# Second graph's features in place of zero products, weight combinations on GpSimd, and a third visit in two parts

## The chip, the cores and the metric

The kernel runs on one core of a Trainium2 chip. Its engines run beside each other and wait for one another by semaphores: TensorE (PE, with its weight loads PEld) multiplies matrices into PSUM, VectorE (DVE) and ScalarE (ACT) work on PSUM and SBUF, GpSimd (POOL) works on SBUF, SyncE (SP) issues DMAs. The metric is the time on the device in microseconds (us). Three runs of the kernel before gave a median of 2787.26 us (2787.23 to 2788.1).

## The reference

Two layers over 64 graphs of 256 nodes with 512 features, all in float32. Layer 0 is a graph attention with 8 heads of 64 units, layer 1 a dot-product attention to which the adjacency is added. Both add their input and end in a layer normalization. The mask is all ones, and `adjacency_mat` and `distance_mat` of layer 1 are both `adj`.

```python
# layer 0
feats = einsum('bnf,hfu->bhnu', x, W)
e_self, e_neigh = einsum('bhnu,hu->bhn', feats, a_self), einsum('bhnu,hu->bhn', feats, a_neigh)
dense = leaky_relu(e_self[..., :, None] + e_neigh[..., None, :], 0.2) - 1e10 * (1 - adj)
x = layernorm(x + relu(einsum('bhij,bhju->bhiu', softmax(dense), feats) + b))
# layer 1
q, k, v = split(x @ W_qkv)
attn = softmax(q @ k.T / 8, masked) * 0.33 + 0.33 * adj + 0.33 * exp(-adj)
x = layernorm(x + (attn @ v) @ W_out + b_out)
```

## The kernel before

**Tiling.** A graph's 256 nodes are T = 2 tiles of 128 rows. The 512 features are C = 4 tiles. Heads come in two groups of HG = 4. Every matmul is issued as two halves of 64 columns (`halved`, L82 to 87), so most PE rows of the profile carry L87 whatever they belong to.

**Seven products.** From graph 2 on, and for q, k, v and the output projection of every graph, a product of 2 x 2 blocks is done with seven block products in place of eight (`seven`, `seven_rows`). They are called p1 to p7. Each needs a sum of blocks of its left side (`left_factors`, the tiles xC, hC, oC, on DVE) and a combination of blocks of the weights. The seven results lie in three PSUM banks: "alone" (p2), "pair" (p5, then p3) and "chain" (p1, p6, p7, p4 one on top of the other). ACT copies the chain bank out after each of its four products, and the next one of the chain waits for that copy. `add` (`qk_add`, `v_add`) adds another bank on DVE.

**Weight combinations.** They are made once, in the start: `combine` (L286 to 299) for q and k, four instructions of 128x1024; `right_factors` (L235 to 247) for v (`wv_sb`, through `CW[0](3)`), for layer 0 (`wf_sb`) and for the output projection (`wo_sb`), four instructions each of 128x512 or 128x528. All sixteen are on DVE.

**Layer 0 of a graph** (`proj0`, `attend0`). For graphs 0 and 1 `features(t, g)` makes the features of a tile and a group of heads directly; `logits` and `copied` take them out of PSUM on DVE; `maxima`, `clamped`, `columns` and `factors` make the exponentials of the logits, one part as a column per head (`CCOL`), one spread over all partitions by matmuls with a selector (`GB`). `aT` transposes the adjacency block by block on DVE, and `far` makes from it two exponentials on ACT. `weights(h)` is one DVE instruction per tile (L767) that makes the unnormalized attention of head h, `scaled(h)` scales the features on ACT (L725), `product(g, t)` multiplies both on PE (L790), `rec0` and `norm0` divide, `end`, `squares` and `norm` are residual and layer normalization, with small steps on POOL (L385 to 406). `shared` makes for layer 1 the part of the attention that comes from the adjacency, on DVE. From graph 2 on the spread exponentials go through DRAM: `rows`, `shift` and `broadcast` write a row tensor gs and read it back on all partitions as gb.

**Zero products.** `keep_busy(dst, n)` (L453 to 456) issues n matmuls of zeros whose result nobody reads. The start has four places: eight in `attention_vectors`, eight and two in `maxima` for graph 0, and six in `busy` for graph 1.

**Order.** The order of the work on each engine is written out by hand: `do(stage, b, step)` runs a step, and `in_order()` chains every instruction to the one before it on its engine. Each engine works its instructions in that order, and so does SP with the DMAs. `start` does all of graph 0's layer 0 and half of graph 1's; `second_beside_first` runs graph 1 beside layer 1 of graph 0; then come, for b = 2 to 62, `attention0_beside_projections1(b)` and `attention1_beside_projections0(b)`, and `end`. The third visit of the change is the first of these two for b = 2.

**Buffers.** Tiles of one tag share as many buffers as `bufs` says. A tile's first writer waits until the last reader of the tile that it replaces is done. Single buffers that matter here: `xb` (an x in blocks, `load`), `adj` (an adjacency in blocks, `load_adj`), `adjT`, `v0` (the features of a graph), `gb`. PSUM has four slots of tag `mm` and two larger ones of tag `sc`.

**Loads.** x and adj are loaded by four DMAs each (`load_blocks`, L119 to 124) on SP, with 128-byte pieces.

Of the kernel before, what the change touches and what calls it, by code (L numbers as in the profile page):

```python
# [17 lines left out]
def kernel(  # L18
# [163 lines left out]
    load_wf(nc.sync, 1)  # L182

    sel = work.tile([P, H + 1, P], FT, tag="rb", name="sel", bufs=1)
    nc.vector.memset(sel[:, H, :], 1.0)
    load_adj(0)
# [48 lines left out]
    def right_factors(w, w12, steps=range(4)):  # L235

        w11, w21, w22, m1, m2, m3, m4 = w
        for i in steps:
            if i == 0:
                nc.vector.tensor_add(m3, w22, w12)  # L240
            elif i == 1:
                nc.vector.tensor_sub(m2, m3, w11)
            elif i == 2:
                nc.vector.tensor_sub(m1, w11, w12)
            else:
                nc.vector.tensor_sub(m4, w21, m2)
        in_order()
# [17 lines left out]
    def load_weights1():  # L265
# [20 lines left out]
        def combine(part):  # L286
            q1, q2, s1, s2, s3, s4, k2 = wqk_sb
            if part == 0:
                nc.vector.tensor_add(s1, wk1, k2)
            elif part == 4:  # L290
                nc.vector.tensor_sub(s2, s1, q1)
            elif part == 1:
                nc.vector.tensor_sub(s3, q1, wk1)
            elif part == 2:
                nc.vector.tensor_sub(s4, q2, s2)
            else:
                right_factors(wv_sb, wv12)
                return
            in_order()
# [196 lines left out]
    def proj0(b):  # L496
# [4 lines left out]
        V0[b] = work.tile([P, T, H, UX], FT, tag="v0", name=f"v0_{b}", bufs=1)  # L501
# [120 lines left out]
        def maxima(part=None):  # L622

            if part == 1:
                matmul(ROW["max"], sel[:H, H, :], ROW["diag"], start=True, stop=True)
                if b == 0:
                    keep_busy(WA[1][:, 0, :2], 2)
# [6 lines left out]
            if b == 0:  # L634
                keep_busy(WA[1][:, 0, :2], 8)
# [654 lines left out]
    def start():  # L1290
# [32 lines left out]
        for t in range(T):  # L1323
            do("proj0", 0, "features", t, 1, 3)
        do("proj0", 0, "aT")
        do("proj0", 0, "far", 0)
        CW[0] = load_weights1()
        load_adj(1)
        do("proj0", 0, "logits", 1)
        do("proj0", 0, "cleared")  # L1330
        do("proj0", 0, "maxima")
        do("proj0", 0, "copied", 0, 0)
        do("proj0", 0, "copied", 1, 0)
        do("proj0", 0, "maxima", 1)
        do("proj0", 0, "clamped")
        do("proj0", 0, "columns")
        for h in range(HG):
# [4 lines left out]
        do("proj0", 0, "factors", HG, HG)  # L1342
        for t in range(T):
            do("attend0", 0, "product", 0, t)
        do("turned", 1, "xT")
        do("proj0", 0, "copied", 0, 1)
        do("proj0", 0, "copied", 1, 1)
        load(2)
        do("attend0", 0, "rec0", 0)
        for h in range(HG, H):  # L1350
            do("proj0", 0, "scaled", h)
        masks(1)
        masks(2)
        do("attend0", 0, "norm0", 0, 0)
        do("attend0", 0, "norm0", 0, 1)
        do("proj0", 0, "far", 1)
        for t in range(T):
            do("proj0", 1, "features", t, 0)
        for h in range(HG, H):
            do("attend0", 0, "weights", h)  # L1360
        for t in range(T):
            do("attend0", 0, "product", 1, t)
        do("proj0", 1, "cleared")
        do("proj0", 1, "logits", 0)
        CW[0](0)
        do("attend0", 0, "rec0", 1)
        CW[0](4)
        for t in range(T):
            do("attend0", 0, "norm0", 1, t)
            do("proj0", 1, "features", t, 1)  # L1370
# [4 lines left out]
        do("proj0", 1, "copied", 0, 0)  # L1375
        do("proj0", 1, "copied", 1, 0)
# [12 lines left out]
        do("proj0", 0, "shared", 0)  # L1389
        do("proj0", 1, "aT")  # L1390
        CW[0](1)
        CW[0](2)
        right_factors(wf_sb, wf12, (0,))
        do("proj1", 0, "qk", "p1")
        do("proj1", 0, "from_rows", 1)
        do("proj1", 0, "blocks")
        load_rows(1)
        do("proj0", 1, "far", 0)
        do("proj1", 0, "qk", "p2")
        do("proj1", 0, "hC")  # L1400
        do("proj1", 0, "qk_add", 11)
        do("proj1", 0, "qk", "p6")
        for h in range(HG):
            do("proj0", 1, "scaled", h)
            do("attend0", 1, "weights", h)
        do("proj0", 0, "shared", 1)
# [3 lines left out]
        do("proj0", 1, "factors", HG, HG)  # L1410
        do("proj1", 0, "qk_add", 22)
        for h in range(HG, H):
            do("proj0", 1, "scaled", h)
        for h in range(HG, H):
            do("attend0", 1, "weights", h)
        do("proj0", 1, "far", 1)
        load_adj(2)
        do("proj1", 0, "qk", "p4")

    def second_beside_first():  # L1420
# [3 lines left out]
        for g in range(2):  # L1424
            for t in range(T):
                do("attend0", b, "product", g, t)
        CW[0](3)
# [18 lines left out]
        right_factors(wf_sb, wf12, (1, 2))  # L1446
# [3 lines left out]
        right_factors(wf_sb, wf12, (3,))  # L1450
# [49 lines left out]
    def attention0_beside_projections1(b):  # L1500
# [17 lines left out]
        for h in range(HG, H):  # L1518
            do("proj0", b, "scaled", h)
        do("proj1", b - 1, "qk", "p5")  # L1520
        for h in range(HG, H):
            do("attend0", b, "weights", h)
        do("proj1", b - 1, "qk", "p7")
        if 2 < b < NB - 1:
            do("turned", b + 1, "xC")
        do("proj1", b - 1, "qk_add", 22)
        for g in range(2):
            for t in range(T):
                do("attend0", b, "product", g, t)
        do("attend0", b, "rec0", 0)  # L1530
# [3 lines left out]
        if b == 2:  # L1534
            do("turned", 3, "xT")
# [3 lines left out]
        do("attend1", b - 2, "weights", 0, 1)  # L1539
        for t in range(T):  # L1540
            do("attend0", b, "norm0", 0, t)
        do("proj1", b - 1, "qk", "p4")
        for t in range(T):
            do("attend0", b, "norm0", 1, t)
        do("proj1", b - 1, "qk", "p3")
        do("attend1", b - 2, "weights", 1, 1)
        do("proj1", b - 1, "qk_add", 12)
        do("attend0", b, "end")
        do("proj1", b - 1, "values", "p1")
        do("proj1", b - 1, "values", "p2")  # L1550
        do("proj1", b - 1, "v_add", 11)
        do("attend1", b - 3, "residual")
# [3 lines left out]
        do("proj1", b - 1, "v_add", 22)  # L1556
        for t in range(T):
# [238 lines left out]
    load(1)  # L1796
# [55 lines left out]
```

## Time and profile before

| | |
|---|---|
| median of three runs | 2787.26 us |
| profiled execution | 2787.98 us |
| its span, first to last instruction | 2786.2 us |
| PE busy | 2773.7 us, 100% |
| DVE busy | 2567.0 us, 92% |
| ACT busy | 1798.0 us, 65% |
| POOL busy | 416.7 us, 15% |
| mean granted clock of TensorE | 0.999 |

A row of the timeline reads: start in us from the span's start, length in us, engine, line of the kernel, operation, output<-input by the program's names, shapes, and xN for N instructions merged into the row. In square brackets stands the idle time of the engine just before, and what ended it. Rows of groups give, after the bar, busy us and the mean ns of one instruction, then the idle time ahead of them. Rows of windows give, after the window and its length, the busy us of PE, PEld, DVE, ACT and POOL, the granted clock, the busy share of the DMA engines and GB/s. Matmuls are pipelined, so the rows of two neighbours can overlap by some 0.1 us.

### The profile page before, as it was taken

What the parts mean: (1) busy time and instruction counts of PE and PEld (TensorE: products, weight loads), DVE (VectorE), ACT (ScalarE), POOL (GpSimd) and SP (SyncE); (2) the same over time, 40 slices, a digit from 0 to 9 for tenths busy, and PEclk for the clock granted to TensorE, in tenths of its full rate; (3) what the DMA queues carried; (4) which work ended last, traced back from release to release, by engine and by line L of the source; (5) the groups of instructions that cost most, each with busy time, mean ns of one, the idle gap of its engine ahead of it and who ended that gap; (6) DMA issues with size and microseconds to landing.
All of it is one profiled execution on the core that took longest, in us unless ns stands there. A gap on an engine that the chain in (4) does not pass through costs nothing.

```text
span 2786.2 us, 93446 instructions
## 1 busy us (share of the span) xinstructions
PE 2773.7 (100%) x38576; PEld 2197.5 (79%) x38576; DVE 2567.0 (92%) x5281; ACT 1798.0 (65%) x5057; POOL 416.7 (15%) x1027
## 2 busy tenths in 40 slices
PE   9999999999999999999999999999999999999998
PEld 7778778788787887887877877878788878788786
DVE  7999999999999999999999999999999999999996
ACT  4566666666666666666666666666666666666664
POOL 1111111111111111111111111111111111111110
PEclk9999999999999999999999999999999999999999
DMA  6444545445445444454454454544544545545432
GB/s 143 124 106 138 134 128 144 124 129 142 120 136 140 124 140 124 135 146 118 133 141 120 139 131 130 145 124 128 145 116 138 138 126 142 124 132 146 116 119 80
DMA packets 778389, 362.57 MB, mean 130 GB/s; under 512 B 694767, under 2 KB 696303, under 8 KB 761966
## 3 DMA queue, kind: packets, MB, share of 16 engines
q1 hardware_dynamic: 775854, 356.07, 47.8%
q8 instruction: 306, 5.01, 0.7%
q14 instruction: 117, 0.96, 0.1%
q10 hardware_dynamic: 2112, 0.52, 0.1%
HBM read 288.11 MB, written 68.13 MB: 128 GB/s over the span
## 4 chain that ended last, share of the span: by engine, by line
PE 98%; DVE 1%; ACT 0%; DMA 0%; issue 0%; POOL 0%; SPq 0%; POOLq 0%; DVEq 0%; ACTq 0%
PE pq_p L87 28%; PE po_p L87 14%; PE pf_p L87 14%; PE pv_p L87 14%; PE av L790 9%; PE pz L951 8%; PE av L1078 8%; PE pd L988 2%; PE pf L87 0%; PE po L87 0%; DMA gb<-gs 0%; PE pg L663 0%; ACT x L811 0%; PE common L1157 0%; PE raw L1142 0%
## 5 line engine op out<-in xcount | busy, mean ns | idle before, releaser
L87 PE MATMUL pq_p<-hC,wqk_sb 128*64 128x128 f32 x8192 | 470.0, 273 | 0.5 <-ACT qk L348 0.5
L87 PEld LDWEIGHTS pq_p<-hC,wqk_sb 128*64 128x64 f32 x8192 | 448.7, 137 | 2.0 <-ACT qk L348 1.0
L767 DVE SCALAR_TENSOR_TENSOR pT<-gb,ccol,at 128x256 f32<-128x256 f32 x992 | 403.1, 478 | 17.3 <-ACT ccol L677 17.3
L87 PE MATMUL pq_p<-hT,wqk_sb 128*64 128x128 f32 x6144 | 358.2, 273 | 0.8 <-DVE hT L130 0.8
L972 ACT ACTIVATE p<-pz,hide 128x512 f32<-128x512 f32 (+1 forms) x640 | 339.3, 623 | 29.3 <-PE pz L951 29.3
L87 PEld LDWEIGHTS pq_p<-hT,wqk_sb 128*64 128x64 f32 x6144 | 342.1, 137 | 11.1 <-PE po_p L87 1.2
L1059 DVE TENSOR_TENSOR p<-p,rb 128x1024 f32<-128x1024 f32 x252 | 299.1, 1207 | 2.4 <-DMA rb<-rs 2.4
L1068 DVE TENSOR_TENSOR p<-p,ct 128x1024 f32<-128x1024 f32 x252 | 299.4, 1208 | 0.1
L811 ACT ACTIVATE x<-av,rec 128x64 f32<-128x64 f32 x1024 | 224.7, 335 | 62.2 <-DVE rec L803 62.2
L790 PE MATMUL av<-v,pT 128*64 128x65 f32 x8192 | 253.4, 222 | 1.6 <-issue 0.9
L725 ACT ACTIVATE v<-v 128x64 f32<-128x64 f32 x1024 | 251.2, 336 | 3.8 <-DVE v L716 3.7
L87 PE MATMUL pf_p<-wf_sb,xC 128*64 128x264 f32 x1984 | 253.6, 386 | 0.0
L790 PEld LDWEIGHTS av<-v,pT 128*64 128x64 f32 x8192 | 249.5, 138 | 3.9 <-issue 2.7
L402 POOL TENSOR_SCALAR rstd_l<-rstd_l 128x2 f32<-128x2 f32 (+1 forms) x128 | 93.9, 734 | 1048.8 <-ACT junk L391 1048.8
L348 ACT COPY qk<-pq_p 128x512 f32<-128x512 f32 x256 | 149.1, 582 | 153.9 <-PE pq_p L87 150.8
L87 PE MATMUL pv_p<-wv_sb,hC 128*64 128x256 f32 x2048 | 243.7, 379 | 0.0
L348 ACT COPY v<-pv_p 128x256 f32<-128x256 f32 x256 | 95.5, 373 | 223.8 <-PE pv_p L87 223.5
L951 PE MATMUL pz<-qk 64*128 64x256 f32 x2048 | 239.4, 383 | 0.0
L87 PE MATMUL po_p<-wo_sb,oC 128*64 128x256 f32 x2016 | 239.2, 379 | 0.0
L1078 PE MATMUL av<-p,v 128*64 128x256 f32 x2016 | 229.1, 379 | 0.0
L951 PEld LDWEIGHTS pz<-qk 64*128 64x128 f32 x2048 | 192.2, 186 | 45.9 <-issue 25.6
L980 DVE SCALAR_TENSOR_TENSOR both<-p 128x512 f32<-128x512 f32 x256 | 173.1, 677 | 41.4 <-ACT p L972 41.4
(181 smaller groups left out, 4549.2 us busy)
## 6 DMA issues: line engine op xcount, KB each, us to landing
rb<-rs SPq DMA_DIRECT2D x63, 1024.0 KB
gb<-gs SPq DMA_DIRECT2D x62, 1028.0 KB
hs<-x SPq DMA_DIRECT2D x64, 512.0 KB
xb<-in_x_dram SPq DMA_DIRECT2D x252, 128.0 KB
x<-in_x_dram SPq DMA_DIRECT2D x63, 512.0 KB
y<-hs SPq DMA_DIRECT2D x63, 512.0 KB
out_dram<-y SPq DMA_DIRECT2D x63, 512.0 KB
hb<-hs SPq DMA_DIRECT2D x248, 128.0 KB
```

Source lines behind the costliest of these rows:

```text
L87: matmul(dst[cols], lhsT[:, cols], rhs, **flags)
L348: nc.scalar.copy(out[COPIES[p]], dst)
L725: nc.scalar.activation(v[:, :U], v[:, :U], AF.Copy, scale=v[:, U : U + 1])
L767: nc.vector.scalar_tensor_tensor(pT[h][:, j, :], GB[b][h], CCOL[b][:, j, h : h + 1], AT[b][:, j, :], op0=ALU.max, op1=ALU.mult,)
L790: matmul(av[r * half : (r + 1) * half, k, :], pT[h][:, j, i : i + half], V0[b][:, j, h, :UA], start=(j == 0), stop=(j == T - 1),)
L811: nc.scalar.activation(X1[b][:, t, h * U : (h + 1) * U], av[:, k, :U], AF.Copy, scale=REC0[g][:, t, k : k + 1],)
L951: matmul(pz[r][:, j, :], QK[b][rows, g, 1, j * P : (j + 1) * P], QK[b][rows, g, 0, :], start=True, stop=True,)
L972: nc.scalar.activation(to, of, AF.Exp, bias=hide[:, j, b : b + 1], scale=U**-0.5)
L980: nc.vector.scalar_tensor_tensor(both[g], p[:, :, 0, :], TINY, p[:, :, 1, :], op0=ALU.add, op1=ALU.add)
L1059: nc.vector.tensor_mul(p, p, REC[b][:, k : k + 2, g // 2, :] .unsqueeze(2) .to_broadcast([P, 2, T, N]),)
L1068: nc.vector.tensor_add(p, p, CT[b].unsqueeze(1).to_broadcast([P, 2, T, N]))
L1078: matmul(av[0][r * U : (r + 1) * U, g % 2, :], V1[b][:, j, 2 * g + r, :], PROBS[b][g][:, r, j, :], start=(j == 0), stop=(j == T - 1),)
```

## The change

Five things are changed; everything from b = 3 on is as it was.

1. Graph 1's x is loaded ahead of adjacency 0 on SP (before: after it, just before `start`), and transposed (`turned`) before graph 0's maxima.
2. The eight and two zero products of `maxima` for graph 0 go. Graph 1's `features` of group 0 are issued at two places in graph 0's layer 0: tile 0 behind the maxima, tile 1 behind the factors. Graph 1's features lie in the buffer of `gb`.
3. All sixteen weight combinations are issued on POOL, those of q, k, v and layer 0 in `start`, those of the output projection where they were.
4. Steps are moved in `start`: `aT` of graph 0 behind the maxima, `aT` of graph 1 ahead of its second logits, `shared` of graph 0 into graph 0's layer 0, all eight `scaled` of graph 1 in one run.
5. For b = 2, p4 and p3 of the q/k product stand between the two groups of `product`, and the later weights, scalings and additions are ordered for that.

```diff
     load_wf(nc.sync, 1)
+    load(1)
+    load_adj(0)
...
-    load_adj(0)
...
             if i == 0:
-                nc.vector.tensor_add(m3, w22, w12)
+                nc.gpsimd.tensor_add(m3, w22, w12)
...
             if part == 0:
-                nc.vector.tensor_add(s1, wk1, k2)
+                nc.gpsimd.tensor_add(s1, wk1, k2)
...
-        V0[b] = work.tile([P, T, H, UX], FT, tag="v0", name=f"v0_{b}", bufs=1)
+        tag = "gb" if b == 1 else "v0"
+        V0[b] = work.tile([P, T, H, UX], FT, tag=tag, name=f"v0_{b}", bufs=1)
...
-                if b == 0:
-                    keep_busy(WA[1][:, 0, :2], 2)
...
-            if b == 0:
-                keep_busy(WA[1][:, 0, :2], 8)
...
             do("proj0", 0, "features", t, 1, 3)
+        do("turned", 1, "xT")
+        do("proj0", 0, "copied", 0, 0)
+        do("proj0", 0, "copied", 1, 0)
+        CW[0] = load_weights1()
+        load_adj(1)
+        do("proj0", 0, "cleared")
+        masks(1)
+        do("proj0", 0, "logits", 1)
+        do("proj0", 0, "maxima")
+        masks(2)
+        do("proj0", 1, "features", 0, 0)
         do("proj0", 0, "aT")
         do("proj0", 0, "far", 0)
...
         do("proj0", 0, "factors", HG, HG)
+        do("proj0", 1, "features", 1, 0)
         for t in range(T):
             do("attend0", 0, "product", 0, t)
...
+            do("proj0", 1, "features", t, 1)
         do("proj0", 1, "cleared")
-        do("proj0", 1, "logits", 0)
         CW[0](0)
+        CW[0](4)
         do("attend0", 0, "rec0", 1)
-        CW[0](4)
+        do("proj0", 0, "shared", 1)
...
-        do("proj0", 1, "copied", 0, 0)
-        do("proj0", 1, "copied", 1, 0)
+        do("proj0", 1, "aT")
         do("proj0", 1, "logits", 1)
...
-        right_factors(wf_sb, wf12, (0,))
+        right_factors(wf_sb, wf12)
+        CW[0](3)
+        do("proj0", 1, "far", 0)
+        do("proj0", 1, "factors", HG, HG)
+        for h in range(H):
+            do("proj0", 1, "scaled", h)
         do("proj1", 0, "qk", "p1")
         do("proj1", 0, "from_rows", 1)
         do("proj1", 0, "blocks")
+        for h in range(6):
+            do("attend0", 1, "weights", h)
...
+        for t in range(T):
+            do("attend0", b, "product", 0, t)
         do("proj1", 0, "qk", "p4")
...
         do("proj1", b - 1, "qk", "p7")
+        if b == 2:
+            do("attend0", b, "weights", HG)
+            do("proj1", b - 1, "qk_add", 22)
+            for h in range(HG + 1, H):
+                do("attend0", b, "weights", h)
+            for h in range(HG, H):
+                do("proj0", b, "scaled", h)
...
         for g in range(2):
             for t in range(T):
                 do("attend0", b, "product", g, t)
+            if b == 2 and g == 0:
+                do("proj1", 1, "qk", "p4")
+                do("proj1", 1, "qk", "p3")
+                do("proj1", 1, "qk_add", 12)
```

## The prediction

> **What bounds the kernel now.** First the page's busy table and chain, to see which engine sets the end.
>
> ```profile
> PE 2773.7 (100%) x38576; PEld 2197.5 (79%) x38576; DVE 2567.0 (92%) x5281; ACT 1798.0 (65%) x5057; POOL 416.7 (15%) x1027
> PE 98%; DVE 1%; ACT 0%; DMA 0%; issue 0%; POOL 0%; SPq 0%; POOLq 0%; DVEq 0%; ACTq 0%
> ```
>
> TensorE is idle for 12.5 us of 2786.2, 7 of them in the last 46. From graph 3's visit on the code is unchanged and PE is full. So the change can gain only what it removes of PE work and of PE stalls in the first 125 us. Next, PE in order of time at the start.
>
> ```profile
> 18.44 1.95 PE L456 MATMUL pa_bc<-rowmask 128*128 128x128 f32 x16
> ...
> 20.64 0.71 PE L456 MATMUL pa_bc<-rowmask 128*128 128x128 f32 x4
> ...
> 36.83 0.75 PE L90 MATMUL pr<-ident,lg 128*8 128x128 f32 x4
> 37.42 1.50 PE L456 MATMUL pg<-rowmask 128*128 128x128 f32 x12
> 39.06 0.66 PE L90 MATMUL ph<-ident,x 128*128 128x128 f32 x4
> ```
>
> The first two L456 rows are the zero products that go. From start to start of their followers they hold PE for 20.32-18.44 = 1.88 and 21.19-20.64 = 0.55: 2.43 us. The row at 36.83 is where the second graph's maxima begin. Last, graph 2 (the third visit), in DVE and PE order of time.
>
> ```profile
> 87.67 0.19 DVE L670 TENSOR_TENSOR nd<-v,gb 128x16 f32<-128x16 f32 x1 [1.81 <-DMA gb<-gs]
> ...
> 88.40 3.21 DVE L767 SCALAR_TENSOR_TENSOR pT<-gb,ccol,at 128x256 f32<-128x256 f32 x8
> ...
> 88.73 1.97 PE L87 MATMUL pq_p<-hC,wqk_sb 128*64 128x128 f32 x32 [0.51 <-ACT qk L348]
> ...
> 90.53 6.26 PE L790 MATMUL av<-v,pT 128*64 128x65 f32 x128
> ...
> 92.13 3.25 DVE L767 SCALAR_TENSOR_TENSOR pT<-gb,ccol,at 128x256 f32<-128x256 f32 x8
> ```
>
> The 128 products take 6.26 us; the same ones for graph 1, and in every later visit, take 3.90. PE follows DVE's weights head by head and loses 2.36 us.
>
> **The start, step by step.** Graph 1's features for group 0 (two blocks of 16 matmuls, 1.95 us each) move ahead of graph 0's maxima and of product 0; PE work is otherwise kept. They need graph 1's transposed x. Its four loads move ahead of adj 0's on SP: from the issue at 11.41-14.78 to 8.00-11.4. Counting bytes in one-microsecond windows in order of issue, all that is ahead of x 1 (1.89 MB) is through at 13.0 and x 1 (0.52 MB more) at 16.7, 1.9 us after its last issue. So x 1 lands near 13.4, and DVE, free at 15.16, transposes it (1.24) by 16.4; the two copies (0.73), the mask transpose (0.38) and the logits come before PE ends the features at 17.85. No wait. adj 0 lands near 16.3; its transpose is now wanted at 19.5: hidden, with 3 us to spare. The PSUM slots for the mask and the new features come free by those copies. The mask's two transposes (0.33) only move. Graph 1's features buffer takes the space of gb, which nothing writes before 81.87: no cost.
>
> PE would thus be 2.43 us early at 36.83, at 34.4. But DVE's transpose of adj 1, at 41.08 before, now stands ahead of logits 1 and maxima 1, and its load keeps its place on SP:
>
> ```profile
> 30.71 2.67 SPq L123 DMA_DIRECT2D adj<-in_adj_dram  x4
> ```
>
> SP is in one stream of issues from 4.6 us to 38, so nothing brings this forward: it ends at 33.38. Landing: bytes counted give 34.3, plus 1.9 us gives 35.3; I take 35.1. Then transpose (0.7) and first logits (0.2): PE starts the maxima at 36.05, not 34.4. A **new stall of 1.6 us** takes the place of two thirds of the gain; 0.78 stays, and 0.23 more since the normalized tile (L90 ph, which waited for ACT) is now early. Queued behind the waiting transpose on DVE are the logits, the maximum and the copies; PE and ACT wait for those. The parts of shared that come earlier on DVE (0.68, 0.29, 0.87 from 29.6) lie where it waits for product 1 or ACT's norm0: nothing. Start: **0.9 to 1.0 gained**; ends 0.3 (landing 35.7) and 2.4 (no wait).
>
> From there to 60 us PE order changes but not its sum. The tightest place is p6, which needs hC: ACT now does all 16 scalings (two rows of 2.02) ahead of the copies of p1 and hT. Counted from factors at 39.96 in old time: ACT is free at 45.6 (0.7 and 4.0 after its column step at 40.9), PE ends p1 at 45.7; copies 1.2 us, three sums on DVE 1.1: p6 at 48.1, where PE gets to at 48.2 (two factor blocks 3.8, p1 1.9, ph 0.6, p2 1.97). Cost 0, up to 0.5. The six weights ahead of hC (4.8 us from 41.6) end at 46.4, before hT is there.
>
> **Weights by GpSimd.** Sixteen DVE instructions go to POOL. The row for POOL is this one:
>
> ```profile
> L467 POOL TENSOR_TENSOR prod<-wf_sb,a_bc 128x512 f32<-128x512 f32 x3 | 3.5, 1192 | 5.4 <-ACT a_bc L441 5.4
> ```
>
> 1.19 us per 128x512 against DVE's 0.68. So 4 x 2.4 + 4 x 1.23 + 8 x 1.19 = 24 us on an engine that is 15% busy; DVE gets 4 x 1.2 + 4 x 0.7 + 8 x 0.68 = 13 back. The first two (s1, s2) run from 27, when their loads are down, to 31.8, and the LayerNorm step behind them on POOL is wanted at 33.1: hidden. s3, s4, wf and wv follow that step, from 36.9 to 51.4: s3 is ready at 39.3 and wanted by p7 near 49, wv at 62.66, wf at 67: hidden. The two of wo stand ahead of POOL's clearing of grow_sb, at 71.28 before and wanted by DVE at 74.0: POOL is free at 71.35, 2.38 + 0.21 gives 73.94. Just hidden; any slowing goes straight into the gb chain.
>
> Rule against this: the Trainium skill, "GPSIMD Engine Reference", Key points, says GpSimd shares its SBUF interfaces with VectorE and contends with DVE instructions that have two SBUF inputs. The row doesn't test that: beside it DVE ran L467 (one input in PSUM) and reductions, at their usual 0.68. By the row the cost is 0. By the rule the hC sums (0.42 each, both inputs in SBUF) may double, +1.1 at p6, and wo may be late by as much. I take the row and keep +2.2 for the range.
>
> **The third visit.** Weights 0 to 3 end at 91.61 in old time. Product group 0 then has a quarter of its first tile and the second left (1.2 us): 92.8. p4 and p3 (1.75 each) cover DVE's weights 4 to 7, which end at 96.0 behind both additions: PE at 96.3; group 1 (1.9) ends at 98.2, against 100.29. Gain 2.1. Off that: norm0 on ACT now falls beside the copies of the values, and p7 of these waits 0.2; and at the row sums of graph 1's softmax (124.72) PE meets DVE, which is ahead by two wo additions (1.2) and its own waits (0.5), 0.3 less than PE. **1.5 gained**; ends 0 (DVE doesn't keep up) and 2.1. The wait of 0.51 and that for gb stay: they hang on gb's DMA, which starts from PE's last product of graph 2 and moves with it.
>
> **Sum.** 0.9 + 1.5 = 2.4 us. The profiled execution took 2787.98 with a span of 2786.2 (1.8 around it): 2783.8 and 2785.6 after. Its time is 0.7 above the median shown, 2787.26, so the median would be **2784.9**.
>
> **The clock.** The stall on adj 1 stands where zero products used to keep PE going. The end of the trace shows what idleness does (windows of one microsecond; PE, PEld, DVE, ACT, POOL, clock, DMA):
>
> ```profile
> 2779.00:2780.00 1.00, 0.23 (x4) 0.00 (x0) 0.65 (x4) 0.51 (x2) 0.00 (x0) 1.00 0.00 0
> 2781.00:2782.00 1.00, 0.00 (x0) 0.00 (x0) 0.18 (x1) 0.19 (x1) 0.70 (x2) 0.78 1.03 387
> 2782.00:2783.00 1.00, 0.00 (x0) 0.00 (x0) 0.17 (x1) 0.32 (x1) 0.00 (x0) 0.50 0.08 29
> ```
>
> PE stops at 2779.23 and the clock halves near 2781.56, 2.3 us later. The skill ("TensorE: Matmul & The Clock Gate", Part 1) puts the drop at one idle window of some 3.4 us. By the page, 1.6 us of stall costs nothing; by the row, 2.3 us can be enough. The price is seen at the start, where eight zero products take 3.78 us (from 1.04) instead of 1.95, with full rate from about 6.2: some 4 us at half rate, +2. I take 0, since 1.6 is under both.
>
> **Rivals.**
> 1. No stall: adj 1 lands by 34.3, or DVE comes to it later. Start 2.4, total 3.9: 2783.4. For it: the byte count. Against it: SP's last issue at 33.38. Chance 0.15.
> 2. Slower: GpSimd's additions run beside DVE at 2.4 us per 128x512 instead of 1.19. s1 and s2 then end at 36.6, the LayerNorm of graph 0 is 3.5 late and PE waits 1.7 at ph; wo ends 2.3 late and gb with it; hC 1.1. -2.4 + 1.7 + 2.3 + 1.1 = +2.7: 2790. It turns the sign from about 1.9 us each. For it: the rule; against it: the row. Chance 0.15, with a part beyond +5.6 where more is late than I see.
> 3. The clock drops at the stall: +2 to +3 on the likeliest: 2787.4, no change. Chance 0.1.
> 4. The third visit gives nothing, DVE being the bound from gb's landing to 124 us: only the start's 0.9: 2786.4. For it: DVE's 100% in 100-110. Chance 0.15.
>
> The likeliest has 0.45, its own range 2784.0 to 2786.2. A measurement of this kernel tells about 0.2%, 5.6 us, from no change. More than that faster would need all of 2.43, 2.36 and 1.5 of other stalls: 0.03. Slower than that: half of rival 2: 0.08. Range: 2782.7 takes in rival 1; 2788.8 takes in 3, 4 and the milder part of 2.
>
> **What would show it.** The features of graph 1 at about 18.8 where L456 stood; DVE idle before L130 adjT<-adj near 34, released by DMA, and PE idle 1.6 us before pr; POOL rows of 1.19 and 2.4; av for graph 2 in two runs of about 2 to 2.3 us with pq_p between, values p1 near 97.3. Wrong if x 1 lands after 15.7, if the POOL rows are much longer, or if the clock column falls below 1.00 near 36 us.

## The result and the profile after

The changed kernel takes 2794.84 us (median of 14 runs, 2792.58 to 2797.59) against 2788.07 for the kernel before (14 runs, 2787.22 to 2790.88): a ratio of 1.0025, 95% interval 1.0017 to 1.0032. It is slower by 6.8 us, where the prediction said 2784.9 with a range up to 2788.8. The profiled execution has a span of 2793.0 us against 2786.2, also 6.8 more. First the busy table and the chain of the changed kernel:

```profile
PE 2771.4 (99%) x38556; PEld 2199.2 (79%) x38556; DVE 2564.5 (92%) x5265; ACT 1796.0 (64%) x5057; POOL 442.3 (16%) x1043
PE 97%; DVE 1%; POOL 0%; DMA 0%; ACT 0%; issue 0%; SPq 0%; POOLq 0%; DVEq 0%; ACTq 0%
```

PE is busy for 2.3 us less and still ends 6.8 us later: it is now idle for 21.6 us of its span instead of 12.5. Where that idle time is shows in PE's order of time (start, length, what; in brackets the idle time before and what ended it):

```profile
18.17 2.00 PE L87 MATMUL pf<-wf_sb,xT 128*64 128x264 f32 x16
...
32.73 1.09 PE L87 MATMUL pf<-wf_sb,xT 128*64 128x264 f32 x8
36.83 0.60 PE L90 MATMUL pr<-ident,lg 128*8 128x128 f32 x4 [3.02 <-DVE lg L615]
...
41.32 5.38 PE L661 MATMUL pg<-grow_sb,sel 128*128 128x256 f32 x16 [1.79 <-DVE nd L668]
...
53.21 5.46 PE L87 MATMUL pq_p<-hC,wqk_sb 128*64 128x128 f32 x96 [2.14 <-DVE hC L315]
...
100.96 1.74 PE L788 MATMUL av<-v,pT 128*64 128x65 f32 x53
103.39 0.51 PE L788 MATMUL av<-v,pT 128*64 128x65 f32 x10 [0.69 <-issue]
...
117.22 1.11 PE L87 MATMUL pf_p<-wf_sb,xC 128*64 128x264 f32 x8 [1.60 <-DVE v L352]
```

The features stand where the zero products stood, and PE is through with graph 1's features at 33.8. Then come three stalls that the kernel before did not have at these places, 3.02, 1.79 and 2.14 us, all released by DVE, and at 41.32 sixteen factor products that take 5.38 us instead of two blocks of 1.99. Why DVE is late shows in DVE's rows of the changed kernel beside POOL's:

```profile
28.86 2.15 DVE L529 TENSOR_TENSOR ct<-adjT,far 128x512 f32<-128x512 f32 x1
31.12 2.25 DVE L531 TENSOR_SCALAR even<-mf 128x256 f32<-128x256 f32 x1
...
38.85 2.32 DVE L644 TENSOR_SCALAR grow_sb<-grow_sb 8x256 f32<-8x256 f32 x1
...
50.17 1.49 DVE L317 TENSOR_TENSOR hC<-hT 128x256 f32<-128x256 f32 x1
51.59 1.48 DVE L315 TENSOR_TENSOR hC<-hT,hC 128x256 f32<-128x256 f32 x1
```

```profile
28.10 2.37 POOL L290 TENSOR_TENSOR wqk_sb<-wk,wqk_sb 128x1024 f32<-128x1024 f32 x1 [3.54 <-DMA wv_sb<-in_L_gnn_W_qkv_dram]
30.55 2.69 POOL L292 TENSOR_TENSOR wqk_sb<-wqk_sb,wqk_sb 128x1024 f32<-128x1024 f32 x1
...
38.68 2.35 POOL L294 TENSOR_TENSOR wqk_sb<-wqk_sb,wk 128x1024 f32<-128x1024 f32 x1
...
49.95 1.43 POOL L243 TENSOR_TENSOR wv_sb<-wv_sb,wv_sb 128x512 f32<-128x512 f32 x1
51.35 1.44 POOL L245 TENSOR_TENSOR wv_sb<-wv_sb,wv 128x512 f32<-128x512 f32 x1
```

The same four in the kernel before:

```profile
39.40 0.28 DVE L646 TENSOR_SCALAR grow_sb<-grow_sb 8x256 f32<-8x256 f32 x1 [0.30 <-ACT grow_sb L640]
...
40.16 0.68 DVE L527 TENSOR_TENSOR ct<-adjT,far 128x512 f32<-128x512 f32 x1
40.87 0.29 DVE L529 TENSOR_SCALAR even<-mf 128x256 f32<-128x256 f32 x1
...
45.77 0.42 DVE L314 TENSOR_TENSOR hC<-hT,hC 128x256 f32<-128x256 f32 x1
```

Add start and length in the changed kernel: POOL's 30.55 row ends at 33.24 and DVE's 31.12 row (`even`) at 33.37; POOL's 38.68 row ends at 41.03 and DVE's 38.85 row (the clamp, 8 rows by 256 elements) at 41.17. The clamp goes from 0.28 to 2.32, `even` from 0.29 to 2.25, `ct` from 0.68 to 2.15, the hC sums from 0.42 to 1.5. The POOL rows beside them last 2.4 to 2.7 and 1.4 us. So certain DVE instructions wait for the end of GpSimd's instruction, whatever their own size.

### The profile page after: what moved, and what is told of

Its sections match the earlier page's. It is cut to its first block, busy times and chain, and to the rows that moved or that the text cites. A ratio compares the mean times of both kernels' runs of the same rounds, so it can differ in the third digit from the quotient of the medians.

```text
span 2793.0 us, 93415 instructions
## 1 busy us (share of the span) xinstructions
PE 2771.4 (99%) x38556; PEld 2199.2 (79%) x38556; DVE 2564.5 (92%) x5265; ACT 1796.0 (64%) x5057; POOL 442.3 (16%) x1043
## 4 chain that ended last, share of the span: by engine, by line
PE 97%; DVE 1%; POOL 0%; DMA 0%; ACT 0%; issue 0%; SPq 0%; POOLq 0%; DVEq 0%; ACTq 0%
PE pq_p L87 28%; PE po_p L87 14%; PE pv_p L87 14%; PE pf_p L87 14%; PE av L788 8%; PE pz L949 8%; PE av L1076 8%; PE pd L986 2%; DVE pT L765 0%; PE pf L87 0%; PE po L87 0%; PE pg L661 0%; DMA gb<-gs 0%; PE common L1155 0%; PE raw L1140 0%
```

## The experiments

Four theories were at stake. **The lock**: while GpSimd works on SBUF, a DVE instruction of a certain kind stands still until GpSimd's ends, and this is the loss. **Bandwidth**: the two engines share one, so each slows the other in proportion. **The order**: the moved steps (adj 1's transpose ahead of logits 1, weights ahead of hC) are the loss. **The clock**: its fall to half rate behind the new stalls is the loss. Letters in the expectations are those that each expectation defines.

Runs that were made together share their runs of the kernel before. All times in us.

| run | median | before's, made together | ratio, 95% |
|---|---|---|---|
| dve_back | 2791.44 | 2789.32 | 1.0007 [0.9999, 1.0016] |
| pool_only | 2795.14 | 2789.32 | 1.0022 [1.0014, 1.0030] |
| split_only | 2790.07 | 2789.32 | 1.0001 [0.9993, 1.0009] |
| late_adj | 2788.96 | 2788.34 | 1.0004 [0.9996, 1.0012] |
| late_start | 2790.21 | 2788.34 | 1.0007 [0.9999, 1.0015] |
| no_zero | 2788.41 | 2788.34 | 1.0001 [0.9992, 1.0009] |
| after_fed | 2795.68 | 2788.44 | 1.0027 [1.0016, 1.0038] |
| wo_pool | 2791.86 | 2788.44 | 1.0010 [1.0004, 1.0017] |

The first loads of an execution land up to 1 us earlier or later: the 16 products of graph 0's features that start at 15.90 in the profile before start at 14.97 in split_only, whose start is the same. The next table therefore gives PE's place counted from that row, less the same for the kernel before. Positive is later. after_again is the changed kernel traced a second time. Each row is one trace. The two of the changed kernel agree within 0.1 us up to graph 0's values and within 0.4 behind them; after_fed, whose code is that of the kernel after up to the second maxima, stands there 0.8 apart from it.

| | second maxima | factors | graph 0's first values | graph 1's first values | row sums (L988) |
|---|---|---|---|---|---|
| before, from that row | 20.93 | 24.06 | 45.03 | 84.39 | 108.82 |
| after | +0.41 | +1.77 | +5.18 | +3.81 | +6.27 |
| after_again | +0.49 | +1.85 | +5.26 | +3.45 | +5.91 |
| pool_only | -0.01 | +1.38 | +5.24 | +6.36 | +6.74 |
| dve_back | +0.17 | -0.34 | +0.19 | -1.47 | +0.13 |
| split_only | -0.01 | -0.02 | -0.02 | -0.92 | +0.64 |
| late_adj | -1.27 | -1.29 | -0.06 | -1.96 | -0.35 |
| late_start | -2.68 | -0.39 | +0.92 | +0.73 | +0.94 |
| no_zero | -0.67 | -0.68 | -0.68 | -1.10 | -0.90 |
| after_fed | -0.42 | +2.07 | +4.26 | +2.90 | +5.36 |
| wo_pool | +0.47 | +1.25 | +1.78 | +0.05 | +2.46 |

**The engine alone (pool_only).** The kernel before, with one part of the change: the engine of the sixteen combinations, at their old places.

```diff
-                nc.vector.tensor_add(m3, w22, w12)
+                nc.gpsimd.tensor_add(m3, w22, w12)
...
-                nc.vector.tensor_add(s1, wk1, k2)
+                nc.gpsimd.tensor_add(s1, wk1, k2)
...
```

> The kernel before with nothing changed but the engine of the sixteen weight combinations: GpSimd in place of DVE, at their old places. Theory A: DVE instructions with two SBUF inputs that meet a GpSimd combination last until its end (up to 1.2 to 2.4 us instead of 0.3 to 0.7), and the time is 2 to 7 us above before. Rival B: GpSimd is idle there anyway and DVE has 13 us less to do, so the time is at or below before, within 1 us.

It came out at 2795.14, 5.8 us above the kernel before: about the loss of the whole change (6.8), with nothing else of it. Two rows of it, DVE and PE:

```profile
48.38 1.48 DVE L314 TENSOR_TENSOR hC<-hT,hC 128x256 f32<-128x256 f32 x1
...
50.01 7.13 PE L87 MATMUL pq_p<-hC,wqk_sb 128*64 128x128 f32 x96 [2.22 <-DVE hC L314]
```

The hC sum takes 1.48 instead of 0.42, and PE waits 2.22 us for it at p6. The 7.13 instead of 5.46 is a halved clock, of which more below; it is 1.7 of this run's 5.24 us at graph 0's values.

**The engine undone (dve_back).** The changed kernel with the sixteen on DVE at the places that they had before; the rest of the change stays.

```diff
-                nc.gpsimd.tensor_add(m3, w22, w12)
+                nc.vector.tensor_add(m3, w22, w12)
...
-        right_factors(wf_sb, wf12)
-        CW[0](3)
+        right_factors(wf_sb, wf12, (0,))
...
+        CW[0](3)
         do("attend0", b, "rec0", 0)
```

> The changed kernel with its new order, its features in place of zero products and its third visit in two parts, but all sixteen weight combinations on DVE again, at the places that they had before. Theory A (GpSimd's two-input instructions and DVE instructions that read two tensors of SBUF, or run at double rate, shut each other out for the whole of an instruction): the long rows of DVE (ct 2.15, even 2.25, clamp 2.32, hC 1.4 to 1.5 us) return to 0.68, 0.29, 0.28 and 0.42, the PE waits of 1.8 ahead of pg and 2.1 ahead of hC go, and the median is between 2784.5 and 2788, some 7 to 10 us under the changed kernel. Rival B (the new order is what costs: DVE's transpose of adjacency 1 ahead of the logits, ACT's scalings in one run): PE still waits 3 us ahead of the second maxima and 2 us ahead of hC, and the time stays above 2792.

At graph 0's values PE stands at +0.19 instead of +5.18, so 5.0 us of the loss come and go with the engine: 0.2 of them are there by the maxima, 2.1 by the factors (the clamp), the rest comes with hC. At the row sums it is +0.13 instead of +6.27. The wait ahead of the factors is gone, the one for hC falls from 2.14 to 0.92. But the wait ahead of the maxima stays, 2.77, and here it has a plain cause, in DVE's rows:

```profile
35.64 0.71 DVE L130 STREAM_TRANSPOSE adjT<-adj 128x512 f32<-128x512 f32 x1 [0.75 <-DMA adj<-in_adj_dram]
```

That is the predicted stall on adj 1's load. The median, 2791.44, is higher than expected (2784.5 to 2788). Against its own before the loss falls from 6.8 us to 2.1, and the interval of the ratio, 0.9999 to 1.0016, doesn't tell that from no change.

**The lock by itself (beside).** Five forms of DVE instruction, alone and beside GpSimd:

```python
nc.vector.tensor_add(dc, da, db)
nc.vector.tensor_scalar(sc, sa, 0.5, 1.0, op0=ALU.mult, op1=ALU.add)
nc.vector.tensor_add(go, ps, ga)
nc.vector.transpose(to, ta)
nc.vector.tensor_reduce(ro, ra.rearrange("p (a b) -> p a b", a=8), AX.X, ALU.add)
...
nc.gpsimd.tensor_add(pc, pa, pb)
```

> No part of the computation is done: it measures instructions by themselves, and stores x in place of the result. Five kinds of DVE instruction of 128x512 (addition of two SBUF tensors; multiply-add of one; addition of a PSUM and an SBUF tensor; transpose; reduction) run alone, then beside GpSimd additions of 128x1024 with two inputs, then beside GpSimd multiply-adds of 128x1024 with one input. Theory A: alone 0.68, 0.41, 0.68, 0.70 and 0.68 us; beside two-input GpSimd the first two last up to 2.4 us longer, to the end of the GpSimd instruction in progress, and the other three are as before. Theory C (SBUF bandwidth is shared out): all of DVE's kinds get longer by a similar part, and GpSimd too. By A as I read it, a one-input GpSimd instruction shuts the first two out as well.

DVE and POOL in order of time, the first row with POOL idle, the last with GpSimd at one-input instructions (1.05 to 1.54 us, mean 1.18, none of them alone):

```profile
12.03 0.42 DVE L77 TENSOR_SCALAR one_out<-one_a 128x512 f32<-128x512 f32 x1
...
17.30 31.30 POOL L107 TENSOR_TENSOR pool_out<-pool_a,pool_b 128x1024 f32<-128x1024 f32 x12 [16.86 <-DVE pool_a L103]
17.66 2.56 DVE L77 TENSOR_SCALAR one_out<-one_a 128x512 f32<-128x512 f32 x1
20.14 0.68 DVE L78 TENSOR_TENSOR mixed_out<-ps,mixed_a 128x512 f32<-128x512 f32 x1
20.74 0.69 DVE L79 STREAM_TRANSPOSE turn_out<-turn_a 128x512 f32<-128x512 f32 x1
21.37 0.64 DVE L80 TENSOR_REDUCE sum_out<-sum_a 128x8 f32<-128x512 f32 x1
21.93 1.05 DVE L76 TENSOR_TENSOR two_out<-two_a,two_b 128x512 f32<-128x512 f32 x1
...
56.93 1.27 DVE L77 TENSOR_SCALAR one_out<-one_a 128x512 f32<-128x512 f32 x1
```

The multiply-add with one SBUF input, which alone is the fastest form (0.42 for 512 elements against 0.64 to 0.70 for the others; I call it doubled-rate), goes from 0.42 to 2.56 beside additions that take 2.34 alone, and to 1.27 beside the one-input instructions: it starts 0.4 us behind GpSimd's instruction (17.30, 2.64 long) and waits for its end. The addition of two SBUF tiles goes from 0.68 to 1.05 only because of where it falls: it starts at 21.93, 0.5 us before a GpSimd addition (20.02, 2.41 long) ends, and all its repeats fall so. In the changed kernel `ct`, of the same form, came 1.6 us before the end of one (28.10, 2.37 long) and took 2.15. One input in PSUM, transposes and reductions don't notice. GpSimd's additions take 2.41 and, every second one, behind DVE's addition, 2.64 to 2.68. A shared bandwidth can't make 2.56 out of 0.42 and leave GpSimd near its own time: the lock stands. The Trainium skill has this, in "SBUF — State Buffer", section "SBUF: two separate sides": the port pair that the two share is an exclusive lock, held by whichever comes first for its whole instruction, against DVE instructions in a doubled-rate mode or with two SBUF inputs. The rows above agree; the clamp of 0.28 that became 2.32 is of the first kind.

**The third visit alone (split_only).** The kernel before with one function of the changed one.

```diff
             for t in range(T):
                 do("attend0", b, "product", g, t)
+            if b == 2 and g == 0:
+                do("proj1", 1, "qk", "p4")
+                do("proj1", 1, "qk", "p3")
...
```

> The kernel before with the third visit in two parts and nothing else of the change. By the prediction's sum the 2.36 us that PE loses in the 128 products of graph 2 shrink, and 1.5 us stay gained at the end: median 2785.5 to 2787. If DVE bounds the stretch from gb's landing to the row sums at 125 us anyway, the gain is given back there by waits of PE on DVE and the time is that of before within 0.4 us.

No gain. Up to graph 1's values PE is 0.92 ahead, half of the 2.1 that was counted; the products of the second group are broken by 1.05 us of "issue", for which the trace shows no releaser. Then PE waits for DVE:

```profile
111.50 1.11 PE L87 MATMUL pf_p<-wf_sb,xC 128*64 128x264 f32 x8 [1.23 <-DVE v L351]
...
124.43 1.07 PE L988 MATMUL pd<-both,ones 128*32 128x256 f32 x16
```

At the row sums it is 0.64 behind. This is rival 4 of the prediction: from gb's landing to 124 us DVE sets the end, and what PE gains there it gives back. One thing this run leaves out: the two wo additions, whose 1.2 us the prediction counted as DVE's head start, are still on DVE here; wo_pool below has them on GpSimd.

**The transpose of adj 1 put back (late_adj).** dve_back, with one step behind the factors again.

```diff
-        do("proj0", 1, "aT")
         do("proj0", 1, "logits", 1)
...
         do("proj0", 1, "factors", 0, HG)
+        do("proj0", 1, "aT")
```

> The kernel after with all sixteen combinations on VectorE (as dve_back) and one more step put back: the transpose of adj 1 behind the factors, as in the kernel before. In dve_back VectorE waited 0.75 us for the load of adj 1 (transpose at 35.64) and TensorE 2.8 us for logits 1. Theory D (the load of adj 1 is what is late): the maxima start near 35.4 instead of 36.55, since logits 1 then follow the row squares that end at 34.9; the median falls by about 1.1 us, to 2790.3, at most by 2.2. Rival E (it is the order of VectorE behind ACT's scaling, not the load): the maxima stay within 0.3 us of 36.5 and the median within 0.5 us of dve_back.

The maxima come 1.44 earlier than in dve_back (-1.27 against +0.17), the median, each against its own before, goes from +2.1 to +0.6, as theory D of this expectation said. Two things that stood ahead of logits 1 are gone: DVE's wait for the load of adj 1 (0.75) and the transpose itself (0.71). The rest of the wait, 1.34, is DVE's order: logits 1 stand behind graph 0's row sums. But the 1.27 are gone at graph 0's values (-0.06): PE then waits 1.60 for hC.

**What the removed zero products can give (late_start, no_zero).** late_start has logits 1 ahead of the row sums too, and the third visit whole: of the change only the features in place of the zero products are left. no_zero is the kernel before without the ten zero products and nothing in their place.

```diff
+        do("proj0", 1, "logits", 1)
         for t in range(T):
             do("attend0", 0, "end", tiles[t])
         for t in range(T):
             do("attend0", 0, "squares", tiles[t])
-        do("proj0", 1, "logits", 1)
```

> late_adj with the third visit whole as before and logits 1 ahead of the row sums of graph 0 on VectorE: only the second graph's x and features in place of the zero products are left of the change. If the removed 2.43 us of zero products are worth what was counted, the maxima start at 34.4 to 34.8 and the first values product near 58.5 to 59.0 (before: 60.93), and the median is 1.5 to 2.4 us below the kernel before. Rival (VectorE is the bound from the landing of gb to 124 us and takes it back): earlier by over 1.5 us at the values, within 0.5 us at 127, and the median within 0.8 us of the kernel before.

```diff
-            if b == 0:
-                keep_busy(WA[1][:, 0, :2], 8)
```

> The kernel before without its ten zero products at 18.4 and 20.6 us, nothing put in their place. Theory F (they stand in time in which TensorE would wait for VectorE's logits and maxima): the factors and everything behind them stay within 0.3 us, two stalls of 1.9 and 0.6 us show instead, and the median is within 0.5 us; a fall of the granted clock to 0.5 for 3.4 us in the next ten us would add up to 1.7 us. Rival G (they delay what follows): everything behind them up to 2.4 us earlier, median 2.4 below.

PE's rows of late_start:

```profile
34.23 0.82 PE L90 MATMUL pr<-ident,lg 128*8 128x128 f32 x4
34.89 1.50 PE L457 MATMUL pg<-rowmask 128*128 128x128 f32 x12
38.75 0.66 PE L90 MATMUL ph<-ident,x 128*128 128x128 f32 x4 [2.35 <-ACT x L411]
39.34 0.38 PE L627 MATMUL pr<-diag,sel 8*128 8x8 f32 x2
39.65 5.41 PE L661 MATMUL pg<-grow_sb,sel 128*128 128x256 f32 x16
```

The maxima are 2.68 earlier, all that was counted and a little more (expected: 34.4 to 34.8). And 2.35 of it are lost two rows on: the transpose of graph 0's normalized tile waits for ACT, which waits for that graph's row sums, statistics and POOL's small steps. That chain ends within 0.4 us of where it ended before. Behind the 2.35 us stall the clock halves (5.41 for 16 factor products), and at the values PE is 0.92 late, where both the expectation and its rival had it early. In no_zero PE waits 1.33 us for ACT at the first maxima, where the eight zero products (1.88) stood: they filled a wait for the most part, and leaving out all ten brings PE 0.68 to 1.1 forward, with nothing in their place. At the row sums it is the earliest of the table, but in the median it can't be told from no change; no version here has a lower median than the kernel before that was made with it.

**The halved clock (after_again, after_fed, gaps, stalls).** after_again is the changed kernel traced once more.

> The changed kernel, traced once more. Theory K (the halved clock at 42.5 us comes when a fixed 3.4-us window happens to hold little work of TensorE): with the same stalls of about 3.0, 1.8 and 2.1 us the fall to 0.50 may stand behind another of them, or behind none; if it is there, 16 factor products or the hC products take 1.6 to 1.7 us longer. Rival (it belongs to this place): the clock halves at 42.3 to 42.7 again.

The clock halves at 41.8 there, at 42.5 in the first trace: about the same place. The windows of one microsecond of the first trace (busy us of PE, PEld, DVE, ACT, POOL, then the granted clock):

```profile
41.00:42.00 1.00, 0.68 (x3) 0.66 (x4) 0.25 (x2) 0.72 (x3) 1.00 (x2) 1.00 1.06 303
42.00:43.00 1.00, 1.00 (x5) 0.83 (x5) 0.00 (x0) 1.00 (x5) 1.00 (x1) 0.74 0.84 236
43.00:44.00 1.00, 1.00 (x4) 0.82 (x3) 0.00 (x0) 1.00 (x5) 1.00 (x2) 0.50 1.04 349
...
45.00:46.00 1.00, 1.00 (x4) 0.82 (x3) 1.00 (x3) 1.00 (x5) 1.00 (x1) 0.55 0.36 58
```

PE is busy through all of it: the half rate comes a microsecond after the stall of 1.79 us has ended, and lasts 3.4 us. after_fed puts zero products into that stall.

```diff
         do("proj0", 1, "maxima", 1)
+        do("proj0", 1, "more", 6)
```

> The changed kernel with six zero products more (1.5 us) in TensorE's stall of 1.8 us between the maxima and the factors of graph 1; they take no time that the stall doesn't give. If the halved clock is one of the causes: no fall at 42.5, the factors in 3.7 to 3.9 us instead of 5.38, the first values product near 64.0 instead of 65.70, and a median lower than that of the kernel after by up to 1.7 us (some 2793.1). If it is not: within 0.3 us at the values.

The factors take 3.62, but another fall, at 37.5, came behind the first stall, and PE's wait for hC grew from 2.14 to 2.67. At the values PE is 0.92 earlier than in the kernel after, with no lower median (2795.68). But 0.83 of that are there at the maxima already, before the edit: GpSimd's first combination, which waits for a load, started at 27.85 there and at 28.10 in the kernel after, 0.8 earlier when both are counted from the features row. From the maxima to the values the two need 28.78 and 28.87 us. So this fall costs next to nothing there: PE makes up for it in the wait for hC behind it, and hC comes when GpSimd's combinations let DVE go. The other fall lies ahead of the wait for the clamp. Where no later wait takes it up, a fall costs: 1.7 in pool_only and, below, 1.3 in wo_pool. Two runs then made stalls of set length, 28 each, with 36 to 42 products of 128x256 between them (each is two of PE's rows).

```python
nc.vector.tensor_add(step[:, :256], ps, other[:, :256])
for _ in range(k - 1):
    nc.vector.tensor_add(step, step, other)
nc.vector.tensor_add(moving, step[:, :256], other[:, :256])
```

> Not the reference's computation: 36 to 42 products of 128x128 by 128x256 between stalls of TensorE made by one, two, three and four additions on VectorE (some 1, 1.7, 2.4 and 3.1 us), seven of each. Theory H (the clock is decided by fixed windows of 3.4 us that stand wherever they stand, and falls for one window if TensorE worked less than some 40% of it): falls to 0.50 last 3.4 us each and begin at times that are whole multiples of 3.41 us apart; after stalls of 1 us none, after 1.7 none or one in seven, after 2.4 two to five of seven, after 3.1 five or more. Rival I (it takes an idle stretch of 3.4 us): none at all. Rival J (any stall of 2.3 us): all of the 2.4 and 3.1, none of the shorter.

In gaps the last line copied another tile and slipped ahead of the chain, so all 28 stalls came out at 0.72 to 0.79 us; none lowered the clock, and nothing else follows. In stalls the line is as shown.

> Not the reference's computation: 36 to 42 products of 128x128 by 128x256 between stalls of TensorE made by a chain of three to six additions on VectorE (two to five of them 0.68 us and longer in sum), seven stalls each of about 1.4, 2.1, 2.8 and 3.5 us. Theory H (windows of 3.4 us that stand wherever they stand; half rate for one window when a window was worked less than some 35 to 40%): every fall lasts 3.4 us or a multiple, and falls begin at whole multiples of 3.41 us apart; 1.4: none; 2.1: none to two of seven; 2.8: two to five; 3.5: five to seven. Rival I (an idle stretch of 3.4 us is needed): only the 3.5. Rival J (2.3 us are enough): all of the 2.8 and 3.5, none of the 2.1.

PE's rows there, two blocks behind stalls of 2.43 us that the clock took differently (0.220 and 0.241 us per row), and the first behind one of 1.70:

```profile
52.26 17.10 PE L70 MATMUL ps<-moving,left 128*128 128x256 f32 x78 [1.70 <-DVE moving L77]
...
167.10 15.81 PE L70 MATMUL ps<-moving,left 128*128 128x256 f32 x72 [2.42 <-DVE moving L77]
185.34 18.79 PE L70 MATMUL ps<-moving,left 128*128 128x256 f32 x78 [2.43 <-DVE moving L77]
```

The clock fell at none of seven stalls of 1.70 to 1.78, four of seven of 2.43, five of seven of 3.15 and five of seven of 3.88. The fourteen falls, read in windows of 0.2 us, begin at whole multiples (6, 18, 30, 42, 55, ... 119) of 3.4134 us from the first, to within 0.01. Cutting the time into such windows sorts all 28 stalls without exception: the clock fell at the end of every window in which PE had been idle for 2.15 us or more, and of none in which it had been idle for 1.98 or less. A stall of 3.88 us that was split into 1.95 and 1.93 cost nothing. Theory H holds, I and J fall. The falls in the kernels' own traces fix the same windows there. The clock fell where a window held 2.22 us of idleness (pool_only) or 2.18 (after_fed); in the kernel after the stall of 3.02 was cut into 1.84 and 1.17 and cost nothing. But it also fell behind windows with less: the one that ended at 42.49 in the kernel after held 1.79, the one that ended at 40.66 in late_start 1.50. These two held 8x8 products and 128x128 transposes besides; that such small products hardly count as work is an inference.

**Where the lock costs late (wo_pool).** dve_back with only the four combinations of wo on GpSimd.

```diff
+        engine = nc.gpsimd if w is wo_sb else nc.vector
...
-                nc.vector.tensor_add(m3, w22, w12)
+                engine.tensor_add(m3, w22, w12)
...
```

> dve_back (all combinations on VectorE, the rest of the change kept) with only the four of wo on GpSimd, as in the kernel after: they lie behind 65 us. If the lock costs there too: TensorE's wait for VectorE at the products of graph 3 (p3) grows from 1.2 to about 1.6, the softmax row sums at 124.40 come 0.3 to 1.0 later, median 0.3 to 1.5 above dve_back's 2791.44. If all of the lock's price falls before 62 us: within 0.3 us at 124.4.

In this trace the stall ahead of the maxima, 3.07 us in the same code as dve_back's, did lower the clock (zero products at 2.43 instead of 1.50):

```profile
36.72 1.01 PE L90 MATMUL pr<-ident,lg 128*8 128x128 f32 x4 [3.07 <-DVE lg L616]
37.52 2.43 PE L458 MATMUL pg<-rowmask 128*128 128x128 f32 x12
```

That is +1.59 over dve_back at the values, before any wo combination. From there to the row sums it loses 0.74 more than dve_back. The loss lies behind graph 1's values, and the table repeats it: from there to the row sums split_only, dve_back and late_adj, all with wo on DVE, lose 1.56 to 1.61, and wo_pool and the three traces with all on GpSimd and the visit in two parts (after, after_again, after_fed) 2.41 to 2.46. The median, 2791.86, can't be told from dve_back's. The wait at graph 3's p3 grows from 1.2 to 1.60, as in the kernel after, where the rows of POOL and DVE show why:

```profile
110.92 2.27 POOL L245 TENSOR_TENSOR wo_sb<-wo_sb,wo 128x512 f32<-128x512 f32 x1
113.16 2.25 POOL L247 TENSOR_TENSOR wo_sb<-wo_sb,wo_sb 128x512 f32<-128x512 f32 x1
115.50 1.05 POOL L403 TENSOR_SCALAR rstd_l<-rstd_l 128x2 f32<-128x2 f32 x1
```

```profile
111.97 2.30 DVE L1057 TENSOR_TENSOR p<-p,rb 128x1024 f32<-128x1024 f32 x1
114.20 0.70 DVE L130 STREAM_TRANSPOSE adjT<-adj 128x512 f32<-128x512 f32 x1
114.83 1.66 DVE L1066 TENSOR_TENSOR p<-p,ct 128x1024 f32<-128x1024 f32 x1
```

Here the two hold each other by turns. GpSimd waits for DVE's 128x1024 softmax products: its combinations take 2.27 instead of 1.28 (the two of wo at 75.38), and the small LayerNorm step behind them 1.05, which takes 0.20 alone. And DVE waits for GpSimd's: its products take 2.30 and 1.66 instead of 1.21, and the addition that PE waits for stands behind them.

## Why the prediction was wrong

- **Weights by GpSimd: "by the row the cost is 0 ... I take the row".** This is the step that failed. It cost 5.0 us up to graph 0's values (after against dve_back; 5.2 in pool_only, 1.7 of it a halved clock behind the stall that the lock made) and some 0.8 more with wo. The row taken (POOL's L467 at 1.19) had DVE beside it only in forms that the lock leaves alone: one input in PSUM, and reductions. The upper end kept, 2.2, was too small too, since it only doubled the hC sums. It left out the doubled-rate instructions with one input (the clamp: +2.0; `even`: +2.0), though the sentence of the Trainium skill that it used ("GPSIMD Engine Reference", Key points) names DVE instructions "in a 2-port perf mode", its name for such a doubled rate, beside those with two SBUF inputs. It left out, too, that an instruction is held for the rest of GpSimd's, not slowed by a factor. The profile before already had the hint: POOL's steps of L402 average 734 ns over the run, against 0.20 us for the same step at 109.21; the one at 151.90 took 1.07 beside a DVE product of two SBUF tiles.
- **Rival 2** had the side and the place right, and its mechanism the wrong way round: GpSimd's 128x1024 rows took 2.35 to 2.69 us where 2.4 was counted, and DVE stood. Only the last two of wo took the 2.3 us per 128x512 that the rival gave them.
- **The new stall on adj 1.** The mechanism was right: dve_back shows DVE waiting for that load, until 35.64 where 35.1 was taken, and the stall was 2.77 where 1.6 was. In the changed kernel itself DVE is held by GpSimd and comes only at 35.94; its stall is 3.02. So the start gained nothing (+0.41 at the maxima) where 0.9 was predicted.
- **Zero products.** 2.43 counted, PE was early by that; but the prediction's "0.23 more since the normalized tile is now early" is wrong: late_start shows that tile as the next thing late, for 2.35. Rival 1 (no stall, 2783.4) would have ended there.
- **p6 and hC: "cost 0, up to 0.5".** Without GpSimd the wait is 0.92 in dve_back and 1.60 in late_adj. DVE's weights ahead of hC end at 47.0 and 47.2, not 46.4. With GpSimd it is 2.14.
- **The third visit: 1.5 gained.** In split_only it was 0.92 at graph 1's values and a loss of 0.64 at the row sums. The step that failed is that DVE would be ahead there, by the wo additions taken from it (1.2) and its own waits: with them on DVE PE loses 1.6 us in that stretch, with them on GpSimd 2.4. Rival 4 was right on this part.
- **The clock: cost 0.** The number was right by luck. The clock did fall, behind the stall of 1.79, and cost next to nothing because PE then waited for hC in any case; where no wait took it up, a fall cost 1.3 (wo_pool) and 1.7 (pool_only). Neither the row of 2.3 us nor the idle window of 3.4 us of the Trainium skill ("TensorE: Matmul & The Clock Gate", Part 1) gives the condition: among products of 128x256 a fixed window with 2.15 us of idleness in it was enough, and of the seven stalls of 3.15 and the seven of 3.88 two each brought no fall. The page's other figure, a free-running window of 3413 ns, is what the stalls show (3.4134).

**What stays open.** dve_back's PE is level with the kernel before at the row sums (+0.13), and its median is 2.1 us above, which its interval doesn't tell from no change. Its profiled execution needs 2664.8 us from the row sums to the end, where the kernel before needed 2661.5 in the same code. That stretch varies by itself, from 2661.5 to 2664.8 over the eleven traces of the table, and from 2662.4 to 2664.2 between the two of the changed kernel. The clock isn't the reason in that execution: its trace has no fall between its first and its last few us. What lengthens the stretch in some executions was not looked into. How much work small products count for in the clock's window was not measured either.

## What to carry to other kernels

Moving elementwise work to an idle GpSimd was free here only beside DVE instructions that read PSUM, transpose or reduce; beside a doubled-rate or two-SBUF-input instruction, one of the two stands still until the other's whole instruction ends, so a 0.28 us clamp on the critical path can cost what the longest GpSimd instruction lasts. When zero products or another filler are taken away, follow the chain to the next thing that is late, here a LayerNorm that had not moved, before counting the gain. And a gain for PE in a stretch where DVE is full is given back at PE's next wait for DVE.

## What the runs showed of the hardware

- DVE beside GpSimd additions of 128x1024 (2.34 us): doubled-rate multiply-add 0.42 to 2.56, two SBUF inputs 0.68 to 1.05 when it starts 0.5 us before GpSimd's end (2.15 for `ct` in the changed kernel, 1.6 us before it), PSUM input 0.68, transpose 0.69, reduction 0.64, unchanged. Beside one-input GpSimd instructions (mean 1.18 us): 1.27 and 0.86.
- Between products of 128x256, TensorE's clock was decided at fixed points 3.4134 us apart: at half rate from there if PE was idle for 2.15 us or more of the 3.41, at full rate if for 1.98 or less. In windows that held transposes and 8x8 products besides, 1.79 and 1.50 us of idleness were enough. So a stall of 2.4 us halves it or not by where it falls, and the half rate comes after the stall, while PE is working. Of the fourteen falls thirteen lasted one window and one lasted two: its first window held another 1.2 us of the stall, so going back up seems to ask for more work than staying up.
